# Chunk 0's recurrence on VectorE, its companions in small pieces, and a planner that knows the rhythm of the steps

## The chip, the core and the metric

The kernel runs on one core of a Trainium2 chip. Its engines are TensorE (PE in the profile; its weight loads are the row PEld), VectorE (DVE), ScalarE (ACT), GpSimd (POOL) and the queue processor SyncE (SP). Each engine works through its own list of instructions in order and waits for the others through semaphores: an instruction whose input is not ready holds up everything behind it on its engine. The metric is the device time of one execution in microseconds (us).

## The reference: a recurrent layer, then attention with a mixture of experts

The input x is (4, 1024, 256): 4 sequences (b) of 1024 tokens (t) with 256 channels.

```
h    = layernorm(x)
p, g = h @ W_state.T + b_state,  sigmoid(h @ W_gate.T + b_gate)
s[t] = tanh(p[t] + s[t-1])                       # 1024 steps, one after the other
x    = x + layernorm(g * s)

h    = rms(layernorm(x));  q, k, v: 16 heads of 16;  q and k are RMS-normed
x1   = layernorm(x) + (causal softmax attention) @ wo.T       # first 64 channels unchanged
moe  = the best 2 of 4 experts for each token, weighted
x    = x + layernorm(x1 + moe)
```

The recurrence is the only part in which a token needs the token before it, over all 1024 of them. Attention of a token needs the tokens up to it, so a block of early tokens can go through attention while the recurrence works on later ones.

## The kernel before: how it is staged, and what sets the order

**Chunks.** The 1024 positions are cut into 8 chunks of 128 (index `i`), each holding 128 tokens of all 4 sequences. For every chunk there are these streams of work:

- `projections`: moments and layernorm of the 4 input tiles on DVE (bn_stats L448, bn_aggr L449, Newton iteration for the inverse root L432 to L439, scaling L520), 8 transposes on PE (L462), two copies out of PSUM (L471, one by ACT, one by DVE), four products with `wsg` (L533), and four evictions by DVE into the big tile `keys` (L551 for the states' half, L547 for the gates' half). `keys` serves as the store of the states until the attention's keys replace them.
- `gates`: tanh of the gates' half on ACT, two operations of 128x512 (L566).
- `recurrence`: 128 steps. A step is an add of 128x8 (256 channels of 4 sequences: 128 partitions by 8) on POOL, L582, and a tanh of 128x8 on ACT, L585. The very first step is a tanh alone (L578). The tanh needs the add, and the next add needs the tanh.
- `before`: state times gate (L614, the first 96 columns early, the last 32 after the last step), transposes (L622), layernorm, the residual, a second layernorm and the transposes for the heads. For chunks 0 and 1 the small inverse roots are DVE's, later POOL's.
- `heads`: products with `wqk` (L710), eviction and squares on ACT (L717, L723), RMS norm of q and k, keys and queries (L750, L761), values.
- attention: scores twice (L882, once for the row maxima and once transposed for the exponentials), maxima on DVE (L967, L974), exponentials on ACT (L1023), causal masks on POOL (L1043), sums on PE (L1064), then output projection, gating and the lists of tokens for each pair of experts. Attention of chunk i costs in proportion to i + 1.

After the last chunk the experts run over those lists until the end.

**The planner.** Nothing of this order is left to a scheduler of the compiler. Each stream is a Python generator that yields `Op(engine, cost, prio, reads, ...)` ahead of each piece of work. `Plan.run` keeps a clock for each engine and always takes the waiting operation that could start first, and among equals the one with the lower priority number; the recurrence has -9, the set-up of constants in `once` has 50. What the plan decides is only the order in which instructions stand on each engine; on the chip they start when their inputs are there. Costs are in us; the plan takes 0.21 for an add, 0.21 for a tanh and 0.03 for a hand-over, so 0.48 for a step.

**Constants around the change.** `AT_ONCE = 5` says that the moments of chunks 0 to 4 may be taken at once, while those of a later chunk wait until the attention of chunk 0 is summed (`ev("av", B - 1)`). `fill` puts matmuls without a use (L416) where the plan sees PE wait for longer than `LEAST`, between 60 and 420 us of the plan. `once` is one stream with the constants: the set-up of `ident_h`, `av` and others (L338 to L348) on DVE as soon as chunk 0's states are there, the zeroing of four `pad` tiles by DVE (L363, L364), the scaling of weights (L367 to L369), constants in `values` (L373), small tables, and masks on POOL (L380 to L400).

In every chunk the step is written so:

```
yield Op("POOL", 0.21, -9.0, [last])
nc.gpsimd.tensor_tensor(s, st[:, :, t], prev, ALU.add)
yield Op("ACT", 0.21, -9.0, [ev("s")])
nc.scalar.activation(st[:, :, t], s, AF.Tanh)
```

Of the kernel before, what the change touches and what calls it, by code (L numbers as in the profile page):

```python
# [8 lines left out]
F32 = mybir.dt.float32  # L9
# [4 lines left out]
ALU = mybir.AluOpType  # L14
# [123 lines left out]
AT_ONCE = 5  # L138
# [32 lines left out]
class Op:  # L171
    def __init__(self, eng, cost, prio, reads=(), slots=(), banks=0, lag=0.0, either=(), ahead=0.0):
        self.eng, self.cost, self.prio, self.reads = eng, cost, prio, reads
        self.slots, self.banks, self.lag, self.either = slots, banks, lag, either
        self.ahead = ahead


class Plan:
# [13 lines left out]

    def ev(self, *key):
        return self.events.setdefault(key, Ready())

    def start(self, op):
        t = self.clock[op.eng]
        for r in op.reads:
            t = max(t, r.at + self.HOP)
        if op.either:  # L200
            t = max(t, min(r.at for r in op.either) + self.HOP)
        for s in op.slots:
            t = max(t, s.best()[1])
        for b in self.banks.pick(op.banks):
            t = max(t, self.banks.free[b])
        return t
# [12 lines left out]
    def run(self, streams):  # L219
# [5 lines left out]
        while waiting:  # L225
# [19 lines left out]
            self.end = t + op.cost + op.lag  # L245
            try:
# [6 lines left out]
def sandwich(  # L253
# [77 lines left out]
    def once():  # L331
# [4 lines left out]
        done("loaded")  # L336
        yield Op("DVE", 2.0, 50.0, [ev("st", 0)])
# [21 lines left out]
        for p in pads.tiles:  # L359
            yield Op("DVE", 1.2, 50.0)  # L360


            nc.vector.memset(p, 0.0)  # L363
            nc.vector.memset(p[:, 1, :, HD : HD + 1], 1.0)  # L364
# [11 lines left out]
        for e in range(1, E):  # L376
# [3 lines left out]
        nc.gpsimd.memset(mask, 0.0)  # L380
        nc.gpsimd.affine_select(
            out=mask, in_=mask, pattern=[[-1, P]],
            compare_op=ALU.is_ge, fill=NEG, base=0, channel_multiplier=1,
        )
        nc.gpsimd.memset(late[:, : 3 * P], 0.0)

# [16 lines left out]
        )  # L403
        done("once")

    def fill(until):

        now = plan.clock["PE"]
        if not FILLED[0] <= now <= FILLED[1] or until - now < LEAST:
            return  # L410
        k, = banks.pick(1)
        if banks.free[k] > now:
            return
        n = int((until - now - 0.4) / 0.35)
        for _ in range(n):
            nc.tensor.matmul(banks.tiles[k], lhsT=ident_h, rhs=late, start=True, stop=True)  # L416
        banks.free[k] = max(banks.free[k], now + 0.35 * n)
# [9 lines left out]
    def newton(z, tag):  # L427

        n = z.shape[1]
        y = stat.tile([P, n], F32, tag=tag + "y", name=tag + "y", bufs=1)  # L430
        t = stat.tile([P, n], F32, tag=tag + "t", name=tag + "t", bufs=1)
        nc.vector.tensor_scalar(  # L432
            y.bitcast(I32), z.bitcast(I32), -0.5, float(0x5F3759DF), ALU.mult, ALU.add
        )
        nc.vector.tensor_scalar(z, z, -0.5, None, ALU.mult)
        for _ in range(3):
            nc.vector.tensor_tensor(t, y, y, ALU.mult)
            nc.vector.tensor_tensor(t, t, z, ALU.mult)
            nc.vector.scalar_tensor_tensor(y, t, 1.5, y, ALU.add, ALU.mult)  # L439
        return y  # L440

    def moments(prio, tiles, tag, reads):

        mv = stat.tile([P, len(tiles), 2], F32, tag=tag, name=tag)
        for n, t in enumerate(tiles):
            yield Op("DVE", 0.6, prio, reads)
# [5 lines left out]
    def transposed(prio, srcs, reads, name, ahead=0.0):  # L452
# [14 lines left out]
        for cc, (eng, copy) in enumerate(  # L467
            (("ACT", nc.scalar.copy), ("DVE", nc.vector.tensor_copy))
        ):
            yield Op(eng, 0.65, prio, [ev(name, "in PSUM")])  # L470
            copy(to[:, cc, : n * P], banks.tiles[bs[cc]][:, : n * P])  # L471
# [23 lines left out]
    def projections():  # L495


        for i in range(NI):
            prio = 4.0 * i - 8.0
            while i not in xc_of:  # L500
                yield Op("DVE", 0.0, prio, [ev("x", i)])
            x_c = xcs.tiles[xc_of[i][1]]
            x_rows = [x_c[:, b, :] for b in range(B)]
            mv = yield from moments(
                prio, x_rows, "mv0", [ev("x", i), *([ev("av", B - 1)] if i >= AT_ONCE else [])]
# [3 lines left out]
            if i:  # L509
                yield Op("DVE", 2.2, prio)  # L510
                nc.vector.tensor_scalar(z, mv[:, :, 1], LN_EPS, None, ALU.add)
                r = newton(z, "r0")
# [5 lines left out]
            for b in range(B):  # L518
                yield Op("DVE", 0.35, prio, [ev("r0", i)])
                nc.vector.tensor_scalar(  # L520
                    x_rows[b], x_rows[b], mv[:, b, 0:1], r[:, b : b + 1],
                    ALU.subtract, ALU.mult,
                )
            done("ln", i)
            to, lnT_ = yield from transposed(prio, x_rows, [ev("ln", i)], f"lnT{i}")
# [3 lines left out]
            for half, dc in ((0, 0), (0, 1), (1, 0), (1, 1)):  # L529
# [15 lines left out]
                yield Op("DVE", 0.68, prio, [ev("pp", i, half, dc)])  # L545
                if half:
                    nc.vector.tensor_scalar(  # L547
                        tile, pb, 0.5, hb_g[:, dc : dc + 1], ALU.mult, ALU.add
                    )
                else:  # L550
                    nc.vector.tensor_scalar(tile, pb, b_s[:, dc : dc + 1], None, ALU.add)  # L551
# [17 lines left out]
    def recurrence():  # L569

        prev = None
        for i in range(NI):
            st, _ = states(i)
            last = ev("st", i)
            for t in range(P):
                if prev is None:
                    yield Op("ACT", 0.21, -9.0, [last])
                    nc.scalar.activation(st[:, :, t], st[:, :, t], AF.Tanh)  # L578
                else:
                    yield Op("POOL", 0.21, -9.0, [last])  # L580
                    s = sp.tile([P, NCC * B], F32, tag="s", name="s")
                    nc.gpsimd.tensor_tensor(s, st[:, :, t], prev, ALU.add)  # L582
                    done("s")
                    yield Op("ACT", 0.21, -9.0, [ev("s")])
# [8 lines left out]
            done("rec", i)  # L593

# [1140 lines left out]
```

## Time and profile before

| | us |
|---|---|
| three runs | 1470.53, 1473.57, 1474.31 (median 1473.57) |
| profiled execution | 1475.52, span 1473.8, mean granted TensorE clock 0.948 |
| first tanh of the recurrence / last tanh of chunk 0 ends | 17.33 / 88.11 |
| first add of chunks 1, 2, 3, 4 | 88.2, 171.6, 247.2, 340.2 |
| first add of chunks 5, 6, 7 / last add | 435.0, 533.6, 643.2 / 740.4 |
| first scores / first exponential | 122.5 / 148.3 |

Lines of the profile name the source line, the engine, what is written from what, the shape and the number of instructions. In the list of groups, the busy time and the mean in ns come after the first bar, and the idle time of the engine just before these instructions after the second, with what ended most of it. In the timeline a row begins with its start and its length in us, and ends with the idle time before it. In the table of stretches a row holds the stretch, its length, the busy time of each engine with its number of instructions, the granted TensorE clock as a share of full speed, the share of the DMA engines that was busy, and GB/s. The times of single steps come from counting the adds that had begun by a given moment.

### The profile page before, as it was taken

What the parts mean: (1) busy time and instruction counts of PE and PEld (TensorE: products, weight loads), DVE (VectorE), ACT (ScalarE), POOL (GpSimd) and SP (SyncE); (2) the same over time, 40 slices, a digit from 0 to 9 for tenths busy, and PEclk for the clock granted to TensorE, in tenths of its full rate; (3) what the DMA queues carried; (4) which work ended last, traced back from release to release, by engine and by line L of the source; (5) the groups of instructions that cost most, each with busy time, mean ns of one, the idle gap of its engine ahead of it and who ended that gap; (6) DMA issues with size and microseconds to landing.
All of it is one profiled execution on the core that took longest, in us unless ns stands there. A gap on an engine that the chain in (4) does not pass through costs nothing. (4 is left out here: it accounts for less than half of the span.)

```text
span 1473.8 us, 43265 instructions
## 1 busy us (share of the span) xinstructions
PE 1324.7 (90%) x17491; PEld 1032.5 (70%) x17506; DVE 897.8 (61%) x2725; ACT 709.1 (48%) x2144; POOL 466.0 (32%) x1466
## 2 busy tenths in 40 slices
PE   4578788998998999999999999999899999999994
PEld 2235446666676776787677677887688889888883
DVE  5566578599688788778877887783414312123331
ACT  2445555655765765776665455657122222223220
POOL 2433544534444444334311100111223312114221
PEclk8789899999999989998999999999899999999997
DMA  4010010001000010001000100221222110102100
GB/s 127 26 46 2 2 43 16 17 2 46 3 31 16 3 32 17 3 18 31 3 4 18 31 3 4 68 75 61 63 76 65 54 50 29 37 23 80 53 28 23
DMA packets 35847, 48.96 MB, mean 33 GB/s; under 512 B 7702, under 2 KB 27926, under 8 KB 35606
## 3 DMA queue, kind: packets, MB, share of 16 engines
q1 hardware_dynamic: 28774, 25.20, 5.5%
q0 software_dynamic: 6560, 20.09, 4.8%
q8 instruction: 143, 2.34, 0.7%
q14 instruction: 98, 0.80, 0.2%
q10 hardware_dynamic: 272, 0.52, 0.1%
HBM read 32.34 MB, written 13.73 MB: 31 GB/s over the span
## 5 line engine op out<-in xcount | busy, mean ns | idle before, releaser
L1023 ACT ACTIVATE ex<-bank 128x512 f32<-128x512 f32 (+1 forms) x592 | 326.2, 582 | 152.1 <-PE bank L882 87.2
L882 PE MATMUL bank<-keys,q 32*128 32x128 f32 x4608 | 352.7, 293 | 16.4 <-ACT q L761 3.6
L582 POOL TENSOR_TENSOR s<-keys 128x8 f32<-128x8 f32 x1023 | 223.1, 218 | 384.5 <-ACT keys L585 373.6
L882 PE MATMUL bank<-q,keys 32*128 32x128 f32 x4608 | 334.7, 293 | 6.5 <-ACT ex L1023 4.1
L882 PEld LDWEIGHTS bank<-q,keys 32*128 32x128 f32 x4608 | 273.7, 193 | 77.1 <-issue 42.9
L585 ACT ACTIVATE keys<-s 128x8 f32<-128x8 f32 x1023 | 218.5, 214 | 211.7 <-POOL s L582 209.1
L882 PEld LDWEIGHTS bank<-keys,q 32*128 32x128 f32 x4608 | 293.0, 193 | 35.9 <-DVE nm L974 6.0
L974 DVE TENSOR_REDUCE nm<-bank 128x1 f32<-128x512 f32 (+4 forms) x336 | 203.2, 639 | 51.4 <-PE bank L882 42.9
L967 DVE CUSTOM_DVE_ANT_0 bank<-bank,late 128x512 f32<-128x512 f32 (+2 forms) x320 | 188.4, 623 | 50.2 <-PE bank L882 49.0
L1043 POOL TENSOR_SCALAR_AFFINE_SELECT ex<-ex 128x256 f32<-128x256 f32 (+1 forms) x240 | 102.7, 429 | 261.6 <-ACT ex L1023 260.7
L1064 PE MATMUL av<-ex,values 128*17 128x128 f32 x4608 | 175.1, 282 | 2.2 <-DVE avT L1083 1.1
L1504 PE MATMUL bank<-values,keys 128*128 128x256 f32 x632 | 150.3, 385 | 6.2 <-PEq L1668 3.2
L1064 PEld LDWEIGHTS av<-ex,values 128*17 128x17 f32 x4608 | 110.0, 99 | 39.1 <-issue 15.2
L1504 PEld LDWEIGHTS bank<-values,keys 128*128 128x128 f32 x632 | 119.5, 193 | 23.8 <-issue 3.7
L1564 ACT ACTIVATE keys<-bank 128x256 f32<-128x256 f32 x136 | 52.2, 384 | 156.1 <-PE bank L1504 155.6
L1504 PE MATMUL bank<-keys 128*128 128x256 f32 x384 | 84.8, 379 | 0.0
L1504 PEld LDWEIGHTS bank<-keys 128*128 128x128 f32 x384 | 73.0, 190 | 9.9
L1591 DVE SCALAR_TENSOR_TENSOR rwnext<-av,rwnext 128x192 f32<-128x192 f32 x28 | 10.4, 414 | 101.6 <-PE av L1523 101.6
L533 PE MATMUL bank<-big,wsg 128*128 128x512 f32 x128 | 63.7, 643 | 5.9 <-ACT big L471 5.9
L710 PE MATMUL bank<-wqk,big 128*128 128x512 f32 x128 | 65.2, 638 | 3.2 <-ACT big L471 3.2
L1523 PE MATMUL av<-keys 128*128 128x192 f32 x384 | 66.4, 326 | 0.0
L1564 ACT ACTIVATE hid<-bank 128x256 f32<-128x256 f32 x66 | 25.4, 384 | 85.2 <-PE bank L1504 85.2
(238 smaller groups left out, 1720.2 us busy)
## 6 DMA issues: line engine op xcount, KB each, us to landing
row_d<-xn SPq DMA_DIRECT2D x16, 512.0 KB
xn<-in_x SPq DMA_DIRECT2D x8, 512.0 KB
xc<-in_x SPq DMA_DIRECT2D x7, 512.0 KB
keys<-in_e_l SPq DMA_DIRECT2D x2, 1024.0 KB
keys<-in_e_w SPq DMA_DIRECT2D x2, 512.0 KB
keys<-in_e_down SPq DMA_DIRECT2D x2, 384.0 KB
rwnext<-row_d,ids POOLq DMA_INDIRECT x36, 4.0
xc<-in_x SPq DMA_DIRECT2D x4, 128.0 KB
```

The lines of the kernel that those rows point to most:

```text
L582: nc.gpsimd.tensor_tensor(s, st[:, :, t], prev, ALU.add)
L585: nc.scalar.activation(st[:, :, t], s, AF.Tanh)
L710: nc.tensor.matmul(pqk, lhsT=hT[:, cc, b * P : (b + 1) * P], rhs=wqk[:, cc, :], start=(cc == 0), stop=(cc == NCC - 1),)
L882: nc.tensor.matmul(banks.tiles[pbs[j]][:, m * P : (m + 1) * P], lhsT=k if kind == "sT" else q, rhs=q if kind == "sT" else k, start=(m == 0 ...
L967: nc.vector.tensor_tensor_reduce(out=s_, in0=s_, in1=late[:, 4 * P - w :], scale=-1.0, scalar=FMAX, op0=ALU.add, op1=ALU.min, accum_out=by ...
L974: nc.vector.tensor_reduce(by_slot[:, half, h0:h1, 2 * p + j], banks.tiles[pb][:, m0 * P : m1 * P].rearrange("p (h w) -> p h w", h=h1 - h0) ...
L1023: nc.scalar.activation(exs.tiles[ex[1]][:, j, : step.w], banks.tiles[pb][:, : step.w], AF.Exp)
L1043: nc.gpsimd.affine_select(out=d, in_=d, pattern=pattern, compare_op=ALU.is_ge, fill=0.0, base=0, channel_multiplier=-1,)
L1064: nc.tensor.matmul(av[32 * j : 32 * j + HD + 1, hc, :], lhsT=v_all[:, b, kb, 4 * hc + j, :], rhs=exs.tiles[ex[j // 2][1]][:, j % 2, m * P ...
L1504: nc.tensor.matmul(hb[0].tiles[hb[1]], lhsT=w[:, j, m * P : (m + 1) * P], rhs=src[:, j, :], start=(j == 0), stop=(j == nk - 1),)
L1523: nc.tensor.matmul(ob[0].tiles[ob[1]][:, t, :], lhsT=src[:, j, t * P : (t + 1) * P], rhs=w[:, j, :], start=(j == 0), stop=(j == nk - 1),)
L1564: nc.scalar.activation(to, src, AF.Gelu)
```

## The change

There are four parts, in one diff.

1. **The adds of chunk 0 are VectorE's** (`BY_VECTOR = 1`). Those of chunks 1 to 7 stay on POOL.
2. **What DVE does beside chunk 0's steps is cut small.** For chunks 1 and 2 (`small = 0 < i < AT_ONCE`) moments are taken over halves of 128 columns, the Newton iteration is yielded instruction by instruction, layernorm works on halves, the copy out of PSUM on quarters, and each eviction of a projection becomes four of 128x128. The pads are zeroed by POOL, and the masks are made before the other constants.
3. **`AT_ONCE` is 3**, so that the projections of chunks 3 and 4 also wait for the attention of chunk 0.
4. **The planner knows the rhythm.** A step's two operations carry `every`, the time from one to the next; `Plan.chain` remembers for DVE or POOL and for ACT when the last one ended and when the next is due. Another operation that would begin before the due time and end more than `FITS` after it is moved behind the next step, unless it is longer than the gap anyway and begins right behind a step. The plan's costs of a step become 0.17 (DVE) or 0.24 (POOL) for the add and 0.22 for the tanh, and the step 0.45 or 0.52.

```diff
+BY_VECTOR = 1
+FITS = 0.05
+RIGHT_BEHIND = 0.06
-AT_ONCE = 5
+AT_ONCE = 3
...
 # Plan.start
+        if op.eng in self.chain and not op.every and op.cost:
+            ended, due, cost = self.chain[op.eng]
+            if t < due < t + op.cost - FITS and not (
+                op.cost > due - ended and t <= ended + RIGHT_BEHIND
+            ):
+                t = due + cost
         return t
 # Plan.run
+            if op.every:
+                self.chain[op.eng] = t + op.cost, t + op.every, op.cost
...
 # once: the masks now come first on POOL
+        yield Op("POOL", 1.5, -1.0)
+        nc.gpsimd.memset(mask, 0.0)
+        nc.gpsimd.affine_select(
+            out=mask, in_=mask, pattern=[[-1, P]],
+            compare_op=ALU.is_ge, fill=NEG, base=0, channel_multiplier=1,
+        )
+        nc.gpsimd.memset(late[:, : 3 * P], 0.0)
+        done("masks")
...
-        for p in pads.tiles:
-            yield Op("DVE", 1.2, 50.0)
-            nc.vector.memset(p, 0.0)
-            nc.vector.memset(p[:, 1, :, HD : HD + 1], 1.0)
...
+        for p in pads.tiles:
+            yield Op("POOL", 1.6, 50.0, [ev("st", 0)])
+            nc.gpsimd.memset(p, 0.0)
+            nc.gpsimd.memset(p[:, 1, :, HD : HD + 1], 1.0)
...
 # fill
-        if not FILLED[0] <= now <= FILLED[1] or until - now < LEAST:
+        if not max(FILLED[0], ev("masks").at) <= now <= FILLED[1] or until - now < LEAST:
...
+    def newton_(z, tag, prio, small):
+        for r in newton_steps(z, tag):      # the same instructions, with a yield after each
+            if small:
+                yield Op("DVE", 0.19, prio)
+        return r
...
 # moments
+            if small:
+                st6 = stat.tile([P, 2, 6], F32, tag="st12", name="st12")
+                for k in range(2):
+                    yield Op("DVE", 0.25, prio, reads)
+                    nc.vector.bn_stats(st6[:, k, :], t[:, k * P : (k + 1) * P])
+                yield Op("DVE", 0.19, prio)
+                nc.vector.bn_aggr(mv[:, n, :], st6)
+                continue
...
 # transposed
-            yield Op(eng, 0.65, prio, [ev(name, "in PSUM")])
-            copy(to[:, cc, : n * P], banks.tiles[bs[cc]][:, : n * P])
+            size = P if small and eng == "DVE" else n * P
+            for at in range(0, n * P, size):
+                yield Op(eng, 0.22 if size == P else 0.65, prio, [ev(name, "in PSUM")])
+                copy(to[:, cc, at : at + size], banks.tiles[bs[cc]][:, at : at + size])
...
 # projections
+            small = 0 < i < AT_ONCE
             for b in range(B):
-                yield Op("DVE", 0.35, prio, [ev("r0", i)])
-                nc.vector.tensor_scalar(
-                    x_rows[b], x_rows[b], mv[:, b, 0:1], r[:, b : b + 1],
+                for sl in (slice(0, P), slice(P, C)) if small else (slice(0, C),):
+                    yield Op("DVE", 0.22 if small else 0.35, prio, [ev("r0", i)])
+                    nc.vector.tensor_scalar(
+                        x_rows[b][:, sl], x_rows[b][:, sl], mv[:, b, 0:1], r[:, b : b + 1],
...
-                yield Op("DVE", 0.68, prio, [ev("pp", i, half, dc)])
+                for bs in [slice(b, b + 1) for b in range(B)] if small else [slice(0, B)]:
+                    yield Op("DVE", 0.22 if small else 0.68, prio, [ev("pp", i, half, dc)])
...
 # recurrence
-                    yield Op("POOL", 0.21, -9.0, [last])
+                    eng, name, cost = (
+                        (nc.vector, "DVE", 0.17) if i < BY_VECTOR else (nc.gpsimd, "POOL", 0.24)
+                    )
+                    step = 0.28 + cost
+                    if t == 0:
+                        plan.chain.clear()
+                    yield Op(name, cost, -9.0, [last], every=step)
                     s = sp.tile([P, NCC * B], F32, tag="s", name="s")
-                    nc.gpsimd.tensor_tensor(s, st[:, :, t], prev, ALU.add)
+                    eng.tensor_tensor(s, st[:, :, t], prev, ALU.add)
                     done("s")
-                    yield Op("ACT", 0.21, -9.0, [ev("s")])
+                    yield Op("ACT", 0.22, -9.0, [ev("s")], every=step)
                     nc.scalar.activation(st[:, :, t], s, AF.Tanh)
```

## The prediction, made before the result was known

> **What bounds the kernel now.** I read the engine table and the slices first, then the two groups of the recurrence, then busy time by stretch, then the timeline around one step and around the end of chunk 0. The chain of waits explains only the last 40 us, so it does not help here.
>
> ```profile
> PE 1324.7 (90%) x17491; PEld 1032.5 (70%) x17506; DVE 897.8 (61%) x2725; ACT 709.1 (48%) x2144; POOL 466.0 (32%) x1466
> L582 POOL TENSOR_TENSOR s<-keys 128x8 f32<-128x8 f32 x1023 | 223.1, 218 | 384.5 <-ACT keys L585 373.6
> L585 ACT ACTIVATE keys<-s 128x8 f32<-128x8 f32 x1023 | 218.5, 214 | 211.7 <-POOL s L582 209.1
> ```
>
> TensorE is busy 90% of the span, but not evenly:
>
> ```profile
> 0.00:122.00 122.00, 77.85 (x206) 37.03 (x208) 71.56 (x265) 48.52 (x200) 42.75 (x205) 0.82 0.20 60
> 122.00:250.00 128.00, 100.18 (x966) 67.35 (x972) 90.61 (x287) 71.05 (x274) 59.02 (x232) 0.93 0.06 18
> 250.00:740.00 490.00, 455.64 (x7669) 337.33 (x7678) 392.09 (x1187) 313.02 (x1067) 212.66 (x810) 0.95 0.06 17
> 740.00:1474.00 734.00, 691.07 (x8660) 590.77 (x8660) 343.50 (x989) 276.49 (x606) 151.62 (x222) 0.97 0.14 42
> ```
>
> The columns after the length are busy PE, PEld, DVE, ACT, POOL. The first scores (L882) start at 122.5; the last step of the recurrence is at 740. Until 122 PE lacks 44 us, from 122 to 250 it lacks 28, and the same stretches hold 11.0 and 19.4 us of fill matmuls (L416), which compute nothing. From 250 to 740 only 34 us are idle and 8.3 are fill. So the front is set by the recurrence and the chain behind it; behind it PE is nearly full.
>
> One step, undisturbed, and the end of chunk 0:
>
> ```profile
> 39.31 0.20 POOL L582 TENSOR_TENSOR s<-keys 128x8 f32<-128x8 f32 x1 [0.33 <-ACT keys L585]
> 39.54 0.22 ACT L585 ACTIVATE keys<-s 128x8 f32<-128x8 f32 x1 [0.31 <-POOL s L582]
> 39.84 0.20 POOL L582 TENSOR_TENSOR s<-keys 128x8 f32<-128x8 f32 x1 [0.33 <-ACT keys L585]
> ...
> 88.14 0.42 DVE L614 SCALAR_TENSOR_TENSOR keys<-keys 128x256 f32<-128x256 f32 x1 [2.96 <-ACT keys L585]
> ```
>
> A step takes 0.527 us. Chunk 0 runs from its first tanh at 17.33 to 88.11, which is 127 x 0.527 = 66.9 plus 3.9 of disturbance.
>
> **The change, part by part.** The sum is against the profiled execution (1475.5 us, span 1473.8), which is 1.9 above the median of the three runs.
>
> *(a) A step on VectorE.* The trace has no such add. Nearest row: the Newton products of the same 128x8 shape, 0.165 us (0.16 to 0.19). DVE to ACT takes 0.04 (the eviction L551 ends at 17.29, the tanh starts at 17.33); ACT to DVE takes 0.03 (88.11 to 88.14). With the tanh of 0.215 a step is 0.45. Ends: 0.43, and 0.50 (the 0.19 row and the 0.07 that POOL needs after ACT). 127 steps: 57.2 for 66.9, **-9.7** (-12.3 to -3.4).
>
> *(b) A later start.* In the order of the changed kernel DVE runs its set-up (L338 to L348) before the first add. In the trace that ends at 19.31 and POOL's first add started at 17.62: **+1.7**. On SP the loads of chunks 5 and 6 move from ahead of the first write of row_d to behind the first four copies of the row maxima into q, so a q can only be issued sooner (0.4 us a load). Masks now come first on POOL (0.9 us there), in 5.1 us in which POOL waits for the first moments: nothing. The zeroing of the four pads goes from DVE (0.91 each) to POOL, about 0.93 each by the memsets there (128x128 0.199, 128x1 0.095); POOL has nothing else before chunk 0 ends and the heads need them only at 110: nothing, or 4 us if that cover were gone.
>
> *(c) What does not fit between two adds.* DVE waits at every add, and all that follows on it waits too. Independent operations overlap by about 0.07, so a piece of up to 0.4 us costs nothing; 128-wide pieces are 0.28 (L1244, SBUF) and about 0.35 (a PSUM eviction: 0.747 at 512 wide, less 384 elements at the 1.03 ns by which L974 falls from 0.685 at 512 to 0.289 at 128), which fit. By the order the misfits are: two whole evictions and two whole gates at the start, +1.2; the weights' scaling twice (0.39+0.26+0.2), +0.9; three copies in one gap, +0.3; the small memsets, +0.3; the first 96 columns of L614 (0.96), +0.5; two ACT copies, +0.2. **+3.4.**
>
> *(d) DVE waiting for PE inside the chain.* Before, this cost no step:
>
> ```profile
> 31.47 4.30 PE L533 MATMUL bank<-big,wsg 128*128 128x512 f32 x6 [1.22 <-ACT big L471]
> 34.95 0.75 DVE L551 TENSOR_SCALAR keys<-bank,vec 128x512 f32<-128x512 f32 x1 [1.40 <-PE bank L533]
> ```
>
> The first product of a projection comes 3.5 us after PE starts on it (granted clock 0.70 in this stretch); the next three 1.72 apart. By the order, chunk 1's first eviction comes six adds and their pieces, 3.5 us, after the add beside which ACT copies the transposes; the copy is done after 0.9, so the product needs 4.4: **+0.9**, and **+0.8** for chunk 2. The next products come every 1.72 and four pieces take 1.8: nothing. Ends 0 and 3.4.
>
> Chunk 0: -9.7+1.7+3.4+1.7 = -2.9 against 66.9; the old 3.9 of disturbance goes, so it **ends 6.8 earlier**, at 81.3 (77 to 91).
>
> *(e) Steps of chunks 1 to 7.* Their adds stay on POOL. From 88.2 to 740.4, 895 steps take 652 us, 180 more than at 0.527. The order has 488 other ACT operations between them: 0.37 us each. Changed: 41, 32, 66, 78, 82, 98, 96 by chunk, for 41, 29, 71, 73, 83, 105, 86, so 493: **+1.9**. The gap rule leaves their number per gap nearly as it was, so I give it nothing by itself; each 0.02 us per operation would be 10 us, either way, if PE followed.
>
> *(f) What is left behind the last step.* 302 exponentials stand before it instead of 298. L882 and L1064 hold 581.6 us over 592: 0.98 each, **-3.9**.
>
> By the steps: -6.8+1.9-3.9 = **-8.8**.
>
> *(g) Room on PE.* AT_ONCE 3 moves the projections of chunks 3 and 4 behind the first attention. One is 8.0 (L533) and 1.5 (L462): 19 us leave a stretch with 44 idle. The order: 3 and 4 stand between the attentions of chunks 0 and 1, 5 and 6 later, and 7 within chunk 3's attention, not chunk 2's. Between first score and last step PE must do 19+3.9 more. By the order the first exponential stands 89 steps behind chunk 0 instead of 97, so scores begin 6.8+4.2 earlier and the last step 4.9 earlier: 6 us more time. So idle and fill, 90 us, must shrink by 17. If none does, the end is 17-8.8 = 8 *later*; if all does, -8.8. From 122 to 250, 47 of 128 us are idle or fill, so I let the half that lands there vanish; of the other 8.4, among the 43 of 490, I charge a third: **+2.8**, since most PE waits there are for DVE pads and avT, which other products can fill. Sum **-6.0**: 1469.5 profiled, 1467.5 on the scale of the median.
>
> The rule that speaks against small pieces: L520 takes 0.413 us at 256 wide, L1244 0.281 at 128, so halving costs 0.15 on DVE for each of 16 such pairs, 2.4 us of busy time that (c) finds hidden behind the adds. [...]
>
> **The rivals.**
> 1. *The moved projections do not fit (slower).* Place: PE from 160 to 740. For: 17 us must be found, and PE is at 93% after 250. Against: fill is planned to be dropped where work stands, and 37% is loose before 250. With nothing found 1473.6+8 = 1482, and 1485 where chunk 0 also gives 3 less. It decides once over 13 of the 17 stay unfound: -8.8+13.2 = +4.4.
> 2. *Chunk 0 gains nothing.* A step at 0.50 (57.2 becomes 63.5) costs 6.3 and cancels it, or waits on PE as in (d) at every product. For: DVE is in order and every wait is now in the chain. Against: the handovers of 0.03 and 0.04. Then -8.8+6.8+2.8 = +0.8: about 1474, no change.
> 3. *The steps' rhythm helps too.* The old plan counts 0.48 for a step that takes 0.527; the new counts 0.52. An operation stretch of 0.35 instead of 0.37 is -10, of which PE can give half: 1462, and 1455 with all its room found.
>
> **How the numbers follow.** The three runs span 0.26%, so 0.3% (4.4 us) is what can be told from no change. My forecast, 1459 to 1469: 0.38. Rival 3: 0.12. Rival 2, 1469 to 1478: 0.20. Rival 1, 1478 to 1490: 0.30. Faster 0.50, same 0.20, slower 0.30. Range 1451 to 1485: from chunk 0 at 77 with the rhythm's help (-4 and -12 on 1467.5) to rival 1's most likely part; beyond both ends I leave 2 in 10.
>
> **What would show it.** Right: adds on DVE every 0.45; the last 32 columns of state times gate begun near 81; waits of 0.9 and 0.8 before the first evictions of chunks 1 and 2; the first exponential near 137 (148.3 before); last step near 735; PE idle plus fill from first score to last step near 76. Wrong: a step of 0.50 (a), many DVE waits on PE (d), or an early first exponential with a last step at 740 or later, which would mean that (g) took it back.

## The result and the profile after

The changed kernel takes **1481.11 us** (median of 6 runs, 1476.02 to 1486.57); the kernel before, run beside it, takes 1473.38 (6 runs, 1470.53 to 1476.54). The ratio is 1.0051, with a 95% interval of 1.0034 to 1.0069: 7.7 us slower, where 6 us faster was forecast. The value lies inside the predicted range; the sign is wrong. The profiled execution after took 1479.5 us (span 1477.7), 1.6 below its median; that of before lay 2.1 above its own, so the two profiles differ by only 4 of the 7.7 us. Two kernels of the experiments below, a_norule and b_j, had one execution each far outside the others (6823.68 and 2432.49 us), which their ratios leave out.

The same parts of the page, after the change: the engine table and the groups of the recurrence. The adds of chunk 0 are now a group of DVE, in the third line (from the list of groups by line).

```profile
PE 1337.6 (91%) x17508; PEld 1043.5 (71%) x17526; DVE 917.1 (62%) x2890; ACT 705.9 (48%) x2144; POOL 444.8 (30%) x1347
L643 POOL TENSOR_TENSOR s<-keys 128x8 f32<-128x8 f32 x896 | 196.9, 220 | 419.2 <-ACT keys L646 417.6
```
```profile
L643 DVE TENSOR_TENSOR s<-keys 128x8 f32<-128x8 f32 x127 | 21.8, 172 | 13.6 <-ACT keys L646 11.1
L646 ACT ACTIVATE keys<-s 128x8 f32<-128x8 f32 x1023 | 218.5, 214 | 203.5 <-POOL s L643 164.9 <-DVE s L643 36.4
```

The recurrence does what was forecast. On VectorE an undisturbed step takes 0.455 us; a piece of other work (here moments on 128 columns) starts under each add and is done before the next. This is the timeline of DVE:

```profile
22.68 0.17 DVE L643 TENSOR_TENSOR s<-keys 128x8 f32<-128x8 f32 x1
22.77 0.29 DVE L485 BATCH_NORM_STATS2 st<-xc 128x6 f32<-128x128 f32 x1
23.13 0.17 DVE L643 TENSOR_TENSOR s<-keys 128x8 f32<-128x8 f32 x1
23.23 0.28 DVE L485 BATCH_NORM_STATS2 st<-xc 128x6 f32<-128x128 f32 x1
23.59 0.17 DVE L643 TENSOR_TENSOR s<-keys 128x8 f32<-128x8 f32 x1
...
83.51 0.43 DVE L676 SCALAR_TENSOR_TENSOR keys<-keys 128x256 f32<-128x256 f32 x1 [0.28 <-ACT keys L646]
```

The last line answers to L614 of before, at 88.14: chunk 0 ends 4.6 us earlier. The busy time by stretch (columns: length, busy PE, PEld, DVE, ACT, POOL, granted clock, DMA share, GB/s):

```profile
0.00:122.00 122.00, 73.45 (x250) 36.35 (x254) 80.92 (x397) 51.33 (x208) 23.26 (x91) 0.81 0.17 52
122.00:250.00 128.00, 108.40 (x960) 70.31 (x969) 92.32 (x289) 67.06 (x263) 57.06 (x224) 0.89 0.07 22
250.00:740.00 490.00, 457.16 (x7438) 340.27 (x7443) 391.79 (x1191) 304.49 (x1045) 208.89 (x793) 0.93 0.06 18
```

From 122 to 250 PE is busy 8.2 us more than before, at a clock of 0.89 instead of 0.93. Yet the work falls behind. The table gives the start of some exponentials and of the last step, in us (the n-th execution of the exponential's line, L1023 or L1085, and of the tanh's, L585 or L646); each of the exponentials shown but the last is the first of its chunk:

| | 1st exponential | 17th (chunk 1) | 49th (chunk 2) | 161st (chunk 4) | 592nd (last) | last step |
|---|---|---|---|---|---|---|
| before | 148.3 | 243.9 | 323.4 | 531.6 | 1026.6 | 740.4 |
| after | 139.2 | 242.1 | 329.3 | 543.2 | 1034.9 | 752.7 |

The 9.1 us won at the first exponential are 1.8 at the 17th, and at the 49th the changed kernel is 6 late. They are lost where more projections now stand: the products of chunks 3 and 4 start at 172.8 and 203.7, and those of chunks 5, 6 and 7 at 284, 399 and 520, where before had them at 204, 262 and 392. So the changed kernel has two projections instead of one from 122 to 250, and three instead of two behind that. This is the place that rival 1 of the prediction named.

Where the time goes is read best between the first score and the last exponential, which hold the same attention in every version. Busy time in that stretch (its end is read to 0.2 us), before and then after; the second line of each fence is fill alone, the matmuls that compute nothing (L416, L436):

```profile
122.50:1026.70 904.20, 835.03 (x15197) 627.72 (x15210) 700.01 (x2067) 552.39 (x1677) 308.60 (x1126) 0.96 0.07 22
122.50:1026.70 904.20, 27.76 (x97) 10.80 (x110) 0.96 0.07 22
```
```profile
114.10:1035.10 921.00, 862.74 (x15227) 648.05 (x15243) 717.51 (x2129) 551.30 (x1684) 309.90 (x1131) 0.94 0.08 23
114.10:1035.10 921.00, 25.71 (x79) 9.64 (x94) 0.94 0.08 23
```

The stretch begins 8.4 us earlier and is 16.8 longer. Useful PE work (busy less fill) grows from 807.3 to 837.0, by 29.8 us; idle time and fill together shrink from 96.9 to 84.0, by 13.0. So the room that was counted on is found in part, and more has to go in than was moved. The moved products account for this much (L533 before, then L584 after; between 122 and 600 us):

```profile
122.00:600.00 478.00, 22.57 (x48) 8.54 (x48) 0.94 0.06 18
```
```profile
122.00:600.00 478.00, 38.64 (x80) 14.77 (x80) 0.90 0.07 20
```

That is 16.1; the line of their transposes (L462, then L505) adds 1.8. The stretch holds 48 useful instructions more, which are the 32 product matmuls and 16 transposes that were moved. The remaining 12 us are therefore the same work taking longer on PE: the scores alone grow by 8.0 (406.5 to 414.5) in the stretch. In the groups of the page the mean of a score matmul rises from 293 to 296 ns, with the median at 270 in both.

The last exponential comes 8.3 us late and the end of the span only 3.9: what follows it, the experts, took 442.8 us here and 447.2 before. In the kept traces of versions that compute the same result this last part takes 440.3 to 450.5 us, and nothing in the change explains where in this range a trace falls. A single trace therefore shows what happens up to the last exponential better than it shows the end.

### The profile page after: what moved, and what is told of

It is laid out like the page before. It is cut to its first block, busy times and chain, and to the rows that moved or that the text cites. A ratio compares the mean times of both kernels' runs of the same rounds, so it can differ in the third digit from the quotient of the medians.

```text
span 1477.7 us, 43349 instructions
## 1 busy us (share of the span) xinstructions
PE 1337.6 (91%) x17508; PEld 1043.5 (71%) x17526; DVE 917.1 (62%) x2890; ACT 705.9 (48%) x2144; POOL 444.8 (30%) x1347
## 5 line engine op out<-in xcount | busy, mean ns | idle before, releaser
L1085 ACT ACTIVATE ex<-bank 128x512 f32<-128x512 f32 (+1 forms) x592 | 326.4, 582 | 171.8 <-PE bank L944 119.0
L944 PE MATMUL bank<-keys,q 32*128 32x128 f32 x4608 | 356.3, 296 | 17.9 <-DVE row L704 5.4
L944 PE MATMUL bank<-q,keys 32*128 32x128 f32 x4608 | 341.8, 296 | 8.5 <-ACT ex L1085 4.0
L944 PEld LDWEIGHTS bank<-q,keys 32*128 32x128 f32 x4608 | 279.3, 194 | 78.2 <-issue 37.1
L944 PEld LDWEIGHTS bank<-keys,q 32*128 32x128 f32 x4608 | 296.5, 196 | 38.1 <-DVE nm L1036 7.3
L643 POOL TENSOR_TENSOR s<-keys 128x8 f32<-128x8 f32 x896 | 196.9, 220 | 419.2 <-ACT keys L646 417.6
L646 ACT ACTIVATE keys<-s 128x8 f32<-128x8 f32 x1023 | 218.5, 214 | 203.5 <-POOL s L643 164.9
L1029 DVE CUSTOM_DVE_ANT_0 bank<-bank,late 128x512 f32<-128x512 f32 (+2 forms) x320 | 188.1, 622 | 40.8 <-PE bank L944 38.7
L1566 PE MATMUL bank<-values,keys 128*128 128x256 f32 x632 | 148.3, 381 | 6.2 <-PEq L1730 3.3
L584 PE MATMUL bank<-big,wsg 128*128 128x512 f32 x128 | 64.3, 642 | 0.2 <-DVE big L516 0.2
```

The costliest lines, as they stand in the source:

```text
L643: eng.tensor_tensor(s, st[:, :, t], prev, ALU.add)
L944: nc.tensor.matmul(banks.tiles[pbs[j]][:, m * P : (m + 1) * P], lhsT=k if kind == "sT" else q, rhs=q if kind == "sT" else k, start=(m == 0 ...
L1029: nc.vector.tensor_tensor_reduce(out=s_, in0=s_, in1=late[:, 4 * P - w :], scale=-1.0, scalar=FMAX, op0=ALU.add, op1=ALU.min, accum_out=by ...
L1085: nc.scalar.activation(exs.tiles[ex[1]][:, j, : step.w], banks.tiles[pb][:, : step.w], AF.Exp)
L1566: nc.tensor.matmul(hb[0].tiles[hb[1]], lhsT=w[:, j, m * P : (m + 1) * P], rhs=src[:, j, :], start=(j == 0), stop=(j == nk - 1),)
```

## The experiments

Theory G: what costs is AT_ONCE 3, which takes the projections of chunks 3 and 4 from a stretch where PE idles and makes the later ones land where it is nearly full. Rivals: the gap rule or the adds on VectorE cost more than they bring; the lower granted clock is a cost of its own; the planner only drew an unlucky order. Every ratio below is to the kernel before, run on the same chip (its medians there were 1475.4, 1475.4, 1480.2 and 1475.2 us, in the order of the groups below), with its 95% interval. "Stretch" is first score to last exponential, in the profiled execution.

### First group: one part at a time

**b_at3**, the kernel before with AT_ONCE 3 alone:

```diff
-AT_ONCE = 5
+AT_ONCE = 3
```

> The kernel before with AT_ONCE = 3 and nothing else. Theory P (the two projections moved behind the first attention take room that PE lacks): chunk 0 ends at 88 as before, but the end comes 8 to 15 us later than before, 1481 to 1488. Theory R (the gap rule and the new step costs put other work badly): no more than 3 us from before, 1470 to 1476. Theory S (any replanning of this kernel moves the time by several us, with no single cause): anything from 1465 to 1485.

Measured: 1486.62 us, ratio 1.0083 [1.0054, 1.0113], 11 us slower. The stretch grows from 904.2 to 922.4, nearly as in the changed kernel, and again it is useful work that grows (807.3 to 830.7) and idle time and fill that shrink too little (96.9 to 91.7):

```profile
120.80:1043.20 922.40, 857.39 (x15231) 639.47 (x15246) 717.42 (x2128) 554.32 (x1683) 313.64 (x1130) 0.95 0.08 23
120.80:1043.20 922.40, 26.70 (x83) 10.08 (x98) 0.95 0.08 23
```

The first score comes only 1.7 us earlier than in before (120.8 for 122.5): taking 19 us of PE work out of the front hardly speeds the front.

**a_at5**, the changed kernel with AT_ONCE 5 (the projections of chunks 1 to 4 then all go in small pieces):

```diff
-AT_ONCE = 3
+AT_ONCE = 5
```

> The changed kernel with AT_ONCE = 5: chunks 1 to 4 are projected in small pieces beside the steps of chunk 0. Theory P: the 19 us of PE work are back in the stretch before the first scores; chunk 0 may end some 3 us later (87), but the end comes 8 to 13 us earlier than in the changed kernel, 1468 to 1473. Theory R: 1478 to 1484, as the changed kernel. Theory S: anything from 1465 to 1485.

Measured: 1470.64 us, ratio 0.9969 [0.9947, 0.9990]. The one number turns the change from slower to faster. Together with b_at3 this settles which part of the change loses: AT_ONCE 3, with and without the rest.

The expectation is wrong in one point, though: the moved products are not all back ahead of the first score. In its trace 72 of the products' matmuls (16 for each chunk) stand between the first score and the last exponential, where the changed kernel has 80 and before has 48. They only stand earlier. The last products of chunk 3 start at 130.9 and 134.8 and chunk 4's at 159, and none starts after 315, while the changed kernel has 32 from 399 on. The stretch as a whole, its fill and its projection products:

```profile
116.30:1023.40 907.10, 846.35 (x15196) 634.14 (x15207) 715.85 (x2129) 549.86 (x1676) 309.52 (x1125) 0.96 0.08 23
116.30:1023.40 907.10, 19.73 (x67) 7.93 (x79) 0.96 0.08 23
116.30:1023.40 907.10, 36.08 (x72) 13.51 (x72) 0.96 0.08 23
```

**a_norule**, the changed kernel without the gap rule, and **a_pool**, with chunk 0's adds back on GpSimd:

```diff
-        if op.eng in self.chain and not op.every and op.cost:
+        if False:
```

> The changed kernel without the gap rule in Plan.start; the step costs, the adds of chunk 0 on VectorE, the small pieces and AT_ONCE = 3 stay. Theory P: 1478 to 1484 as the changed kernel, chunk 0 ends 1 to 5 us later since pieces stand in front of steps. Theory R: the loss of chunks 2 to 5 (their first exponentials 6 to 13 us later than before) goes, 1468 to 1474. Theory S: anything from 1465 to 1485.

```diff
-BY_VECTOR = 1
+BY_VECTOR = 0
```

> The changed kernel with BY_VECTOR = 0: chunk 0's adds on POOL too, at 0.527 a step. Chunk 0 ends near 87 instead of 83. Theory P: the 4 us are lost again at the end, 1483 to 1488. If what chunk 0 gains is lost anyway behind it (the first exponential came 9 us earlier but that of chunk 2 was 6 later), 1478 to 1483. Theory R: as the changed kernel, 1478 to 1484.

Measured: 1.0052 [1.0033, 1.0071] and 1.0066 [1.0041, 1.0090], against 1.0051 with both. Neither part is what costs; neither brings anything that these runs can tell either, as long as AT_ONCE is 3. Without the adds on VectorE the first exponential comes 9.1 us later (148.4), and the last one only 3.6 later (1038.5 for 1034.9). Chunk 0 ends at 92.9 there, where 87 was expected and before had 88.1. So what else was changed lengthens chunk 0 by 5 us when its adds are on GpSimd, and the adds on VectorE are worth 9 to 10 us in it rather than the 4.6 that the two main profiles show.

### Second group: which engine's room, and how many chunks

**e_pe** leaves out half of the input channels of the projection products of chunks 3 and 4 (8 of TensorE's us), in the changed kernel's order. **e_dve** takes the moments and the layernorm of these chunks over 16 of the 256 columns and without the Newton rounds. That was expected to save 8 of VectorE's us; its busy time in the stretch falls by 5.5 (717.5 to 712.0). Other data reaches the experts in both, whose work depends on it, so only times up to the last exponential can be compared.

```diff
-                for cc in range(NCC):
+                for cc in range(1 if i in (3, 4) else NCC):
```

> The changed kernel with the same order on every engine, but for chunks 3 and 4 each of the four products of the projection is one matrix product over 128 channels instead of two summed over 256 (half of that work is left out): 8 us less on PE, nothing less on DVE or ACT. If the moved projections cost their room on PE: 5 to 9 us faster than the changed kernel, 1472 to 1477. If they cost through DVE: at most 2 us faster, 1479 to 1483.

```diff
-            nc.vector.bn_stats(st6, t)
+            nc.vector.bn_stats(st6, t[:, :cut])
...
-                for sl in (slice(0, P), slice(P, C)) if small else (slice(0, C),):
+                for sl in (slice(0, P), slice(P, C)) if small else (slice(0, 16 if i in (3, 4) else C),):
```

> The changed kernel with the same order, but for chunks 3 and 4 moments and layernorm are taken over 16 of 256 columns and the Newton iteration is left out: some 4 us less of DVE for each of the two chunks, 8 us in all, PE's work unchanged. If the moved projections cost through DVE: 5 to 8 us faster than the changed kernel, 1473 to 1477. If they cost room on PE: at most 2 us faster, 1479 to 1483.

Measured: the last exponential comes at 1029.8 and 1030.5, for 1034.9, so 5.2 and 4.4 us earlier. (The whole times, 1507.72 and 1476.02 us, are not comparable.) These are single executions, and they do not settle which engine was short. The six runs of the changed kernel alone lie up to 10 us apart. The profiled execution of e_pe was the fastest of its four by 4 us (1503.03, the others 1507.38 to 1508.61), that of e_dve the slowest of its ten (1479.43). And in e_dve, where PE has the same instructions, its busy time less fill still falls from 837.0 to 831.0. That the moved work is paid on both engines is possible, but it is not shown.

**a_at4**, the changed kernel with AT_ONCE 4: only chunk 4's projections go behind the first attention.

```diff
-AT_ONCE = 3
+AT_ONCE = 4
```

> The changed kernel with AT_ONCE = 4: only chunk 4's projection is moved behind the first attention, chunk 3's is done in small pieces beside chunk 0's steps. If each moved projection costs its half: in the middle between AT_ONCE 5 (1470.6) and 3 (1481 to 1482), 1474 to 1478. If the first one is absorbed by the loose stretch before 250 and only the second costs: as AT_ONCE 5, 1469 to 1473.

Measured: 1467.42 us, ratio 0.9952 [0.9938, 0.9966], the best of all and faster than either expectation. Of chunk 3's products half stand ahead of the first score, the others at 130.6 and 134.5, ahead of the first exponential. Still that exponential comes at 138.4 (139.2 after), the first score at 114.9 (114.1): there they cost next to nothing. The stretch is 908.2 us instead of 921.0 (as a whole, fill, and projection products):

```profile
114.90:1023.10 908.20, 847.28 (x15204) 634.58 (x15222) 709.48 (x2106) 550.97 (x1676) 308.61 (x1125) 0.96 0.08 23
114.90:1023.10 908.20, 23.05 (x74) 9.12 (x92) 0.96 0.08 23
114.90:1023.10 908.20, 33.61 (x72) 12.56 (x72) 0.96 0.08 23
```

Idle time and fill are 84.0 there, as in the changed kernel, which thus found no more room although it had 12.8 us more of useful work to place (837.0 for 824.2). Of these 5.0 are projection products (80 matmuls instead of 72); the others are their transposes and, again, other work taking longer.

**a_fill**, the changed kernel with more fill; every engine's order stays, only fill and the numbers of the PSUM banks differ:

```diff
-FILLED = (60.0, 420.0)
-LEAST = 0.8
+FILLED = (60.0, 740.0)
+LEAST = 0.4
```

> The changed kernel with more fill matmuls: up to 740 us of the plan and from waits of 0.4 us on, to see what the granted TensorE clock (0.89 to 0.93 from 122 to 600, where the kernel before had 0.92 to 0.97) is worth. If the lower clock is what costs: mean clock up by 0.01 and 4 to 9 us faster, 1472 to 1477. If the clock only follows the idle time and PE's work is the cause: 1479 to 1485.

Measured: 1473.01 us, ratio 0.9997 [0.9981, 1.0014], 8 us below the changed kernel, with a mean granted clock of 0.952 instead of 0.942. Taken alone it says that the loss is the clock. The whole times of the next two groups do not bear that out.

### Third group: is it the clock, and do the gains add?

**b_fill** and **a_at4_fill** make the same edit on before and on a_at4, again in an unchanged order; **b_at4** is before with AT_ONCE 4; **a_at4_pool** is a_at4 with BY_VECTOR 0.

> The kernel before with fill matmuls allowed from 60 to 740 us and in gaps from 0.4 us, instead of 60 to 420 and 0.8; the recurrence and the projections are untouched. In the changed kernel the same edit added 10 us of fill, raised the mean granted clock from 0.942 to 0.952 and took 8 us off (1481.1 to 1473.0). Theory C (the lower granted clock is a cost of its own, for any order of this work): before, whose clock is 0.948 already and whose stretches from 122 to 430 are at 0.93 to 0.97, has less to win: 2 to 6 us, 1469 to 1473. Theory W (the changed kernel lost its clock because of its own gaps, so fill repairs only that): before is unmoved, within 0.2% of 1475, with the clock at 0.947 to 0.950. If fill delays real products it is 1477 or more.

> The changed kernel with AT_ONCE 4 and with the wider fill. If the two gains add (14 from AT_ONCE 4, 8 from fill): about 1460. If both repair the same loss (with AT_ONCE 4 the clock is already 0.952, from 0.942): 1466 to 1469, the clock no higher than 0.955. Above 1471 would mean that the fill gets in the way of the projections that AT_ONCE 4 brings forward.

> The kernel before with AT_ONCE 4 alone: chunk 4's projections behind the first attention, chunk 3's ahead of it. AT_ONCE 3 alone cost 11 us on before (1486.6 for 1475.4). If the cost goes by the projections moved (8.0 + 1.5 us of PE each): half, 1479 to 1482. If only the second one overfills the stretch, as the changed kernel suggests (AT_ONCE 4 there is no slower than 5): 1473 to 1477. Faster than 1471 would mean that 4 is the better place by itself and that the new parts of the changed kernel gain nothing.

> The changed kernel with AT_ONCE 4 and chunk 0's adds on GpSimd as before (BY_VECTOR 0); small pieces and the gap rule stay. Chunk 0 then ends 9 to 10 us later than with AT_ONCE 4 and the adds on VectorE (first exponential near 148 instead of 138.4). If that gain reaches the end: 1475 to 1477. If it is taken back by the room on TensorE, as with AT_ONCE 3 (where the same edit cost 2.6 us): 1468 to 1471.

| | ratio | first score | stretch | useful | idle and fill | last exponential |
|---|---|---|---|---|---|---|
| b_fill | 0.9991 [0.9971, 1.0011] | 123.0 | 900.1 | 793.3 | 106.8 | 1023.0 |
| a_at4_fill | 0.9956 [0.9937, 0.9976] | 115.3 | 906.3 | 809.4 | 96.9 | 1021.6 |
| b_at4 | 0.9978 [0.9957, 0.9999] | 122.2 | 901.8 | 809.2 | 92.6 | 1023.9 |
| a_at4_pool | 1.0013 [0.9994, 1.0031] | 124.9 | 906.9 | 815.2 | 91.7 | 1031.6 |

More fill gains nothing in the whole time on before (0.9991) nor on a_at4 (0.9956 for 0.9952), although the granted clock of the profiled execution rises to 0.957 in both (from 0.948 and 0.952). On a_at4 this is also what was expected if AT_ONCE 4 and fill repair the same loss. Useful PE time falls by 14 to 15 us, and idle time with fill grows by 10 and 13: in these traces a faster PE mostly waits longer. One projection behind the first attention costs before nothing (0.9978).

With AT_ONCE 4 the adds on VectorE reach the end in this pair: 0.9952 against 1.0013. The stretch is as long with them as without (908.2 and 906.9) and begins 10 us earlier. That is the kind of gain that (a) to (d) forecast; with AT_ONCE 3 it was spent. How much of it another order would keep is open: the next group has one with these adds at 0.9991.

### Fourth group: the clock once more, and the scatter of an order

**b_at3_fill** is b_at3 with the wider fill, in the same order. **a_j**, **a_at4_j** and **b_j** let the planner write another order of the same work, by planning a projection product at a slightly different cost (1.81, 1.83 and 1.86 us):

```diff
-                pp, = yield Op("PE", 1.8, prio, lnT_, banks=1, lag=0.2)
+                pp, = yield Op("PE", 1.81, prio, lnT_, banks=1, lag=0.2)
```

> Before with AT_ONCE 3 and the wider fill (60 to 740 us, gaps from 0.4 us); every engine's order is that of before with AT_ONCE 3, only fill and the numbers of the PSUM banks differ. AT_ONCE 3 alone: +11 us, mean granted clock 0.942 for 0.948. Theory C (the cost of AT_ONCE 3 is the clock that PE loses): the fill takes 6 to 9 us off, as on the changed kernel, ratio to before 1.002 to 1.004, clock 0.950 or more. Theory R (it is room: 19 us of products that have to go somewhere): 0 to 3 us off, ratio 1.006 to 1.009, whatever the clock.

> The changed kernel with a projection product planned at 1.81 us instead of 1.80: the same work, in an order that differs from the 798th product of TensorE on. If AT_ONCE 3 is what costs: within 4 us of the changed kernel, ratio to before 1.003 to 1.008. If the changed kernel only drew an unlucky order: 0.995 to 1.001.

> The changed kernel with AT_ONCE 4 and a projection product planned at 1.83 us instead of 1.80: an order that differs from the 440th product on. If AT_ONCE 4 is what helps: ratio to before 0.993 to 0.998. If the version with 4 only drew a lucky order: 1.000 to 1.005.

> The kernel before with a projection product planned at 1.86 us instead of 1.80: an order that differs from the 609th product on. The scatter of a re-planned order by itself: within 4 us of before, ratio 0.997 to 1.003. If it is outside that, differences of 5 us between single orders say little.

Measured: b_at3_fill 1486.90 us, 1.0077 [1.0049, 1.0104], clock 0.949: nothing gained on b_at3, so by the whole time theory R (room) holds there and theory C (clock) falls. a_j 1489.47 us, 1.0101 [1.0069, 1.0132]; a_at4_j 1472.53 us, 0.9991 [0.9971, 1.0012]; b_j 1471.64 us, 0.9971 [0.9953, 0.9989].

The traces say less clearly that fill buys nothing. In all four pairs the last exponential comes earlier with more fill: 1034.9 to 1028.5 on the changed kernel, 1026.6 to 1023.0 on before, 1022.8 to 1021.6 on a_at4, 1043.2 to 1035.4 on b_at3. In the last three the part behind it is 3.3, 9.2 and 5.7 us longer, which takes the gain back; on the changed kernel it is not. Each is one execution, partly on another chip, so this is a lead and no more.

a_j and a_at4_j lie outside what was expected of them, both on the slow side; b_j is inside. So orders of the same work scatter by 0.3 to 0.5%, 4 to 7 us, and no comparison of two single orders is good to less. What outlasts the scatter, leaving out the versions with more fill: the five orders with AT_ONCE 3 (after, a_j, a_norule, a_pool, b_at3) lie at 1.0051 to 1.0101, mean 1.0071; the seven others (before, b_j, b_at4, a_at4, a_at4_j, a_at4_pool, a_at5) at 0.9952 to 1.0013, mean 0.9982. The two sets don't overlap; the means are 0.9% or 13 us apart. (Of the versions with more fill b_at3_fill, at 1.0077, lies with the first set, but a_fill, at 0.9997, with the second.) In the traces the sets differ in one more way: each of the five has 32 of the projections' product matmuls, those of two chunks, after 350 us, each of the seven 16 or none. This fits a loss that arises where PE is nearly full, but no run moved these products alone.

## Why the prediction was wrong

**(a) The step: right.** 0.455 us measured, 0.45 forecast; the add is 0.172, for 0.165 by its nearest row.

**(b) The later start: right.** The first add started at 19.59 us on DVE, for 17.62 on POOL before: 1.97, forecast 1.7.

**(c), (d) Disturbances inside chunk 0: 1 us too low, and partly by compensation.** From the first add, 127 undisturbed steps would end at 77.4 (19.59 + 127 x 0.455 = 77.37); the state times gate began at 83.51, so 6.1 were lost, where 5.1 were forecast. The two waits for PE, in the timeline of DVE:

```profile
38.99 0.35 DVE L603 TENSOR_SCALAR keys<-bank,vec 128x128 f32<-128x128 f32 x1 [0.96 <-PE bank L584]
...
66.36 0.35 DVE L603 TENSOR_SCALAR keys<-bank,vec 128x128 f32<-128x128 f32 x1 [2.33 <-PE bank L584]
```

The first is 0.96, forecast 0.9. The second is 2.33, forecast 0.8; the add behind it on DVE began at 66.62, though the tanh that it needs had ended at 64.28. PE's timeline gives the rest:

```profile
61.34 0.64 PE L436 MATMUL bank<-late,ident_h 128*128 128x512 bf16 x1
62.20 1.06 PE L436 MATMUL bank<-late,ident_h 128*128 128x512 bf16 x2 [0.22 <-issue]
63.05 4.13 PE L584 MATMUL bank<-big,wsg 128*128 128x512 f32 x6
```

ACT's copy of the transposes was done at 61.54 (60.97 + 0.57), but fill stood in PE's list until 63.05. That the 1.5 us are fill's is read from the order and was not tried by itself. Chunk 0 ended at 83.5, forecast 81.3; the first exponential came at 139.2, forecast 137.

**(e) The steps of chunks 1 to 7: wrong, as a consequence.** Forecast +1.9. From the 128th to the last step it took 668.7 us, for 651.6 before: +17. Less 895 x 0.527 this is 0.40 us for each of the 493 other ACT operations instead of 0.37. The price was taken as a constant of the trace, and it was not one; that later inputs of ACT raised it is argued, not tested. The order of b_at3, where the steps' plan is untouched, shows that ACT's steps are not what loses: there the last step comes at 729.6, 11 us earlier than in before, and the last exponential 16.5 later.

**(f) Exponentials left behind the last step: right.** 302 stand before the last step, as forecast, and from the last step to the last exponential it took 282.3 us, for 286.2 before: the 3.9 forecast. They came off behind a last step at 752.7, though, where 735 was forecast.

**(g) Room on PE: the step that failed.** It charged 2.8 us; the profile shows 14.7 up to the last step. Busy time from the first score to the last step, before and then after, with fill alone in the second lines:

```profile
122.50:740.50 618.00, 556.21 (x8647) 405.17 (x8664) 482.49 (x1470) 383.89 (x1341) 271.94 (x1041) 0.94 0.06 17
122.50:740.50 618.00, 27.76 (x97) 10.80 (x110) 0.94 0.06 17
```
```profile
114.10:752.80 638.70, 583.86 (x8742) 425.37 (x8760) 501.66 (x1532) 385.32 (x1352) 273.49 (x1047) 0.92 0.06 18
114.10:752.80 638.70, 25.71 (x79) 9.64 (x94) 0.92 0.06 18
```

The stretch is 20.7 us longer (618.0 to 638.7), where 6 were forecast. The 14.7 have two parts:

- The prediction put 19 + 3.9 = 22.9 us more work into 6 us more time, so that idle time and fill should shrink by 17 (16.9), of which 2.8 were charged as unfound. They shrank by 9.0 (89.5 to 80.5): 7.9 unfound.
- Useful work grew by 29.7 (528.45 to 558.15), not 22.9: 6.8 us more, for which the prediction had no term. It is the same work done more slowly, as above.

Which half of the room was missing can be read from the stretches at the head, with the fill of the changed kernel:

```profile
122.00:250.00 128.00, 17.77 (x56) 6.78 (x66) 0.89 0.07 22
250.00:740.00 490.00, 7.94 (x23) 2.85 (x28) 0.93 0.06 18
```

Between 122 and 250 idle time and fill go from 47.3 to 37.4 us, so the half that the prediction placed there was found. Between 250 and 740 they go from 42.7 to 40.8, only 1.9 less, where it counted on two thirds of 8.4. Its reason was that other products can fill PE's waits there; PE was 93% busy there before and stays at 93%. That the work for those waits was not ready in them would explain it; this is a guess that no run tests by itself.

With the first score at 114.1 instead of the implied 111.5, 2.6 later, the steps' own sum gives -8.8 + 14.7 + 2.6 = +8.5, and the last exponential came 8.3 later. Most of this agreement is arithmetic, since 14.7 and 2.6 are taken from the same trace; what it tests is (f). The charge of (g) was five times too small.

**The rivals.** Rival 1 was right in place and, partly by luck, in size: 1482 with nothing found, 1481.1 measured. Its condition, over 13 of the 17 unfound, was not met as worded: 7.9 were unfound, and the 6.8 of slower work, which neither rival 1 nor the forecast had, made up the rest. It was given 0.30. The argument that outweighed it, that fill is planned to be dropped where work stands, was weak: fill fell by just 2.1 us (27.8 to 25.7) in the stretch. Rival 2 (chunk 0 gains nothing) and rival 3 (the rhythm helps the steps) both fell: by (a), and by a_norule, which shows no gain from the gap rule.

**The price of small pieces.** The prediction put it at 0.15 us of DVE for each halving, from the rows of L520 and L1244, and took it to be hidden behind the adds. With the adds on GpSimd and AT_ONCE 4, where the pieces hide under no chain on DVE, the small pieces, the gap rule and the rest of the change together stand at 1.0013 against 0.9978 for b_at4, and the first score is 2.7 us later (124.9 for 122.2). That speaks against the pieces, with 5 us, but it lies within the scatter of orders. Under the adds on VectorE, pieces of 0.28 and 0.29 us left the period at 0.455, as the timeline shows.

**What stays open.** Why the same order with more fill was 8 us faster on the changed kernel and no faster on three others (before, a_at4, b_at3), and with it how much of the loss is room and how much is the same work done more slowly. Which engine, PE or VectorE, was short. And whether the change without AT_ONCE 3 beats before: a_at4 and a_at5 do, by 7 and 5 us, but a second order with AT_ONCE 4 is at 0.9991, and b_j, a mere reordering of before, at 0.9971.

## What to carry to other kernels

Idle time on the engine that bounds a stretch was not all room here (idle time and fill shrank by 9.0 of the 16.9 us needed): before work is moved into it, ask which wait each gap belongs to and whether the moved work, with all its engines, is ready in that gap. Ask too what the moved work pushes back in its turn: here chunks 5 to 7 were pushed to where PE was 93% busy. Work that stood where its engine idled anyway was nearly free here, so such work is the last to move: in b_at3 taking 19 us of it out of the front brought 2 us there and cost 18 behind (922.4 for 904.2). And where a planner writes the order, change a cost that should not matter and measure how far the time moves before you believe a difference of half a per cent.

## What the runs showed of the hardware

- **Time went with the granted clock within one program, but a clock raised with fill bought time in one pair of four only.** Over 28 executions of the kernel before on one chip, from 1475.5 to 1485.6 us, the mean granted clock lay between 0.939 and 0.952, and 0.01 of it went with 7.5 us (correlation -0.89). Yet in three of four pairs the wider fill raised the profiled clock by 0.005 to 0.009 and the whole time stayed, as the third and fourth groups show. So the correlation is no price list.
- **A lower clock without longer gaps.** Between the first score and 742 us the timeline of before lists three idle times of PE of 3.0 us or more, the longest 4.09, at a mean clock of 0.94; the changed kernel has none that long, its longest is 2.77, and its mean clock is 0.92. What lowered the clock here, no run settles.
- **On VectorE the chain of adds and tanhs carried short pieces of other work for nothing.** A step of add and tanh on VectorE and ScalarE takes 0.455 us, of which the add is 0.172 and the tanh 0.214, so that the two handovers together take about 0.07; on GpSimd it is 0.527. In the timeline of the changed kernel the 0.455 is the same with a piece of 0.28 or 0.29 us under each add (22.68 to 23.59, two steps) and with none (74.41 to 83.06, 19 steps); with pieces of 0.34 us a step took 0.456 (30.88 to 34.53, eight steps).
